# A graph network on one core: the column table and the attention weights of the attention loops stand in PSUM

## The chip, the cores and the metric

The kernel runs on one core of a Trainium2 chip. A core has a matrix engine (TensorE, PE in the profile), a vector engine (VectorE, DVE), a scalar engine (ScalarE, ACT), a general engine (GpSimd, POOL) and a queue engine (SyncE, SP). Each works off its own instructions in order and waits on semaphores for the others. SBUF is the working memory; PSUM is the small memory that TensorE writes its products into, in eight banks of 512 float32 values for each of 128 partitions. The metric is the device time of one execution in microseconds, and the figure compared is the median over runs.

## The reference

Four layers work on a graph of 3125 nodes with 256 features. Each layer adds a graph part, a mixing part (linear attention over all nodes) and a feed-forward part to the node features. The graph parts of layers 0 and 2 are graph attention over 50,000 edges sorted by destination, with 4 and 8 heads. Cut to what matters:

```
def _L2_gnn_ref(x, edge_index, W, att_src, att_dst, ...):
    xl = (x @ W).reshape(n, H, C)
    a_src = jnp.einsum('nhc,hc->nh', xl, att_src)
    a_dst = jnp.einsum('nhc,hc->nh', xl, att_dst)
    ...                                   # every node is an edge to itself too
    logits = jax.nn.leaky_relu(a_src[src] + a_dst[dst], 0.2)
    seg_max = jax.ops.segment_max(logits, dst, num_segments=n)
    ex = jnp.exp(logits - seg_max[dst])
    denom = jax.ops.segment_sum(ex, dst, num_segments=n)
    alpha = ex / denom[dst]
    msgs = xl[src] * alpha[:, :, None]
    out = jax.ops.segment_sum(msgs, dst, num_segments=n).reshape(n, H * C) + bias
    ...                                   # layer norm over the features
```

The other layers' graph parts are a weighted sum over the edges (layer 1, twice) and three rounds of sums (layer 3).

## The kernel before

Nodes stand in 25 blocks of 128 rows. Edges stand in 416 tiles of 128, each tile within one block of destinations; `self.blk` holds the block of each tile and `self.dl` the place of each edge's destination in its block. Four tiles make a group (`G = 4`), two groups a pair (`Z = 2`), so an attention loop runs over 104 groups, or 52 pairs.

The method `gat` (line 746) does one attention layer. Per group `g` its loop runs these steps; `k` is the number of the pair.

- `fetch(g)` (line 849) issues four gathers on GpSimd (line 533), which bring 128 rows of the table `htab` each from memory into a buffer `msg` of SBUF. There are five such buffers.
- `terms(k)` (line 817) loads a row of destinations, builds a transposed one-hot matrix `ohT` on VectorE (line 823) and copies eight rows of destination terms to `stage` on ScalarE (line 828), each from an offset read from `blk`.
- `look(k, i)` (line 830) multiplies the two on TensorE, four small matmuls per call (line 834), into the PSUM tile `pds[k % 2]`, one bank for even pairs and one for odd ones.
- `weights(k)` (line 837) sums the three bfloat16 parts on VectorE (line 841), forms the logits `z` there (lines 843 to 845) and takes the exponential on ScalarE (line 847) into `alpha`, a tile of SBUF.
- `scale(g)` (line 856) multiplies the gathered messages by `alpha` in place (line 860), copies `alpha` beside them (line 861), and builds the one-hot matrix `oh` of the destinations (`one_hot`, line 537, its instruction on line 540), which compares `dl` with a table of the column numbers 0 to 127, `self.cols`. All three are VectorE's and all operands are in SBUF.
- `sums(g)` (line 865) multiplies `oh` by the messages on TensorE, four matmuls (line 871) into two PSUM buffers named `g`; `add_to` (line 546) adds each product to the block's row of `agg` on VectorE, one group later.

In a turn with an even `g` the pair's steps stand in front of the group's: `weights(k + 1)`, then `terms(k + 2)`; each turn then issues `look(k + 2, g % 2)`, `scale(g)`, `sums(g)` and the additions of the group before. Between turns a generator `steps` issues parts of the mixing computation (matmuls of lines 467, 465 and 504 with their ScalarE and VectorE work), which fill TensorE beside the loop.

The order of the instructions on each engine is not that of the text: a scheduler orders them when the kernel is built, by its own costs, and sets the semaphores. It tracks dependences inside a PSUM tile by bank. Two instructions of different engines that touch one bank of one tile, in which at least one of them writes, are put in order and wait for each other, though they touch different columns.

Layer 1 has a loop of the same make, `gather_sum` (line 552). It runs twice, over the table `c_tab`. In its second run the comparison takes the column table from a PSUM tile named `acc`, and its other long VectorE instructions have an operand in PSUM as well.

Of the kernel before, what the change touches and what calls it, by code (L numbers as in the profile page):

```python
# [9 lines left out]
F32 = mybir.dt.float32  # L10
# [9 lines left out]
P = 128  # L20
# [10 lines left out]
G = 4  # L31
# [20 lines left out]
def bc(ap, shape):  # L52

    idx, full = [], []
    own = list(ap.shape)
    for n in shape:
        if n is None:
            idx.append(slice(None))
            full.append(own.pop(0))
        else:  # L60
            idx.append(None)
            full.append(n)
    assert not own
    return ap[tuple(idx)].to_broadcast(full)


class Net:
# [678 lines left out]
    def gat(self, pool, pre, H, tiny, side, deg=None, after=None, during=None):  # L746

        nc, tc = self.nc, self.tc
# [56 lines left out]
        Z = 2  # L805
        ng = NS // G
        state = {}
        heads = agg[:, :, :D].rearrange("p t (h c) -> p t h c", h=H)
        with ExitStack() as own:
            steps = side(own)  # L810
            msgs = own.enter_context(self.pool("msgs", 5))
            ps = own.enter_context(self.pool("gat_ps", 1, PSUM))

            pds = [ps.tile([P, Z * G, 2, H, 3], F32, name=f"pd{i}") for i in range(2)]

            def terms(k):

                t0, n = k * Z * G, Z * G
                dr = pool.tile([P, n, P], BF16, name="dr")
                rows = self.dl_rows[t0:t0 + n]  # L820
                nc.sync.dma_start(dr, bass.AP(tensor=rows.tensor, offset=rows.offset, ap=[[0, P], [P, n], [1, P]]))
                ohT = pool.tile([P, n, P], BF16, name="ohT")
                nc.vector.tensor_scalar(ohT, dr, self.row, None, op0=ALU.is_equal)
                pd = pds[k % 2]
                rows = pool.tile([P, n, 6 * H], BF16, name="stage")
                for j in range(n):
                    at = self.block_of(t0 + j, ET.Activation) * (6 * H)
                    nc.scalar.copy(rows[:, j, :], dmf[:, bass.ds(at, 6 * H)])  # L828
                state["pd", k] = pd, ohT, rows

            def look(k, i):
                pd, ohT, rows = state["pd", k]
                for j in range(i * G, (i + 1) * G):
                    nc.tensor.matmul(pd[:, j].rearrange("p s h k -> p (s h k)"), ohT[:, j, :], rows[:, j, :],  # L834
                                     start=True, stop=True)

            def weights(k):
                t0, n = k * Z * G, Z * G
                pd4 = state.pop(("pd", k))[0]
                pd = pool.tile([P, n, 2, H], F32, name="pds")  # L840
                nc.vector.tensor_reduce(pd, pd4, axis=AX.X, op=ALU.add)
                z = pool.tile([P, n, H], F32, name="z")
                nc.vector.tensor_tensor(z, ase[:, t0:t0 + n, :], pd[:, :, 0, :], ALU.add)
                nc.vector.scalar_tensor_tensor(z, z, 0.2, z, op0=ALU.mult, op1=ALU.max)
                nc.vector.tensor_tensor(z, z, pd[:, :, 1, :], ALU.subtract)
                al_ = pool.tile([P, n, H], F32, name="alpha")
                nc.scalar.activation(al_, z, AF.Exp)
                state["w", k] = al_

            def fetch(g):  # L850
                msg = msgs.tile([P, G, W], F32, name="msg")
                for j in range(G):
                    self.gather(msg[:, j, :D], htab, g * G + j)
                state["msg", g] = msg

            def scale(g):
                msg = state["msg", g]
                al_ = state["w", g // Z][:, (g % Z) * G:(g % Z + 1) * G, :]
                mh = msg[:, :, :D].rearrange("p j (h c) -> p j h c", h=H)
                nc.vector.tensor_tensor(mh, mh, bc(al_, [None, None, None, C]), ALU.mult)  # L860
                nc.vector.tensor_copy(msg[:, :, D:D + H], al_)
                if deg is not None:
                    nc.vector.memset(msg[:, :, D + H:], 1.0)
                state["oh", g] = self.one_hot(pool, g)

            def sums(g):
                oh, msg = state.pop(("oh", g)), state.pop(("msg", g))
                out = []
                for j in range(G):
                    q = ps.tile([P, 512], F32, name="g", bufs=2)[:, :W]  # L870
                    nc.tensor.matmul(q, oh[:, j, :], msg[:, j, :], start=True, stop=True)  # L871
                    out.append(q)
                state["q", g] = out

            terms(0)
            look(0, 0)
            look(0, 1)
            weights(0)
            terms(1)
            look(1, 0)  # L880
            look(1, 1)
            nc.scalar.activation(ws, ws, AF.Exp)
            nc.vector.tensor_tensor(heads, heads, bc(ws, [None, None, None, C]), ALU.mult)
            nc.vector.tensor_copy(agg[:, :, D:D + H], ws)
            if deg is not None:
                nc.vector.memset(agg[:, :, D + H:], 0.0)
            for g in range(ng + 1):
                if g < ng:
                    fetch(g)
                    k = g // Z  # L890
                    if g % Z == 0:
                        if k + 1 < ng // Z:
                            weights(k + 1)
                        if k + 2 < ng // Z:
                            terms(k + 2)
                    if k + 2 < ng // Z:
                        look(k + 2, g % Z)
                    scale(g)
                    sums(g)
                if g:  # L900
                    self.add_group(agg, g - 1, state.pop(("q", g - 1)))
                if g % 6:
                    next(steps, None)
                if g < ng and during is not None:
                    during(g)
            for _ in steps:
                pass
# [10 lines left out]
        for b in range(0, NB, BB):  # L918
            s = slice(b, b + BB)
# [1583 lines left out]
```

## Time and profile before

| what | value |
|---|---|
| median of 6 runs | 6624.34 us (6580.49 to 6642.68) |
| the profiled execution, its own time | 6648.39 us |
| its span on the core | 6646.6 us |
| mean granted clock of TensorE | 0.849 |
| attention loop of layer 0 | about 572 to 1180 us of the span |
| attention loop of layer 2 | about 4055 to 4710 us of the span |
| second loop of layer 1, column table in PSUM | about 2380 to 3190 us |

The page has a busy time for each engine, a strip of 40 slices, the chain of work that ended last, and groups of instructions with their mean time and what ended the idle time before them. In a group's row, `msg<-msg,alpha` is output and inputs by the program's names; the figure behind the bar is the busy time in microseconds, then the mean of one instruction in nanoseconds, then the idle time before them and its releasers. `issue` is idle time for which no releaser is seen, and `remote` a releaser that the profile does not name.

### The profile page before, as it was taken

How to read it: one execution, taken by the hardware profiler on the slowest of the kernel's cores; microseconds unless marked ns; L12 is line 12 of the kernel's file. 1: busy time of each engine (PE TensorE's matmuls, PEld its weight loads, DVE VectorE, ACT ScalarE, POOL GpSimd, SP SyncE). 2: the span in 40 equal slices, each digit the busy share in tenths (PEclk: the TensorE clock that was granted, in tenths of full speed). 3: DMA queues.
4: the chain of work that ended last, by engine and by line, in shares of the span. 5: the costliest groups of instructions: out<-in, count | busy, mean ns of one | idle time of the engine just before them, and what ended most of it. 6: DMA issues, size and time to landing. Idle time of an engine off the chain costs nothing.

```text
span 6646.6 us, 82827 instructions
## 1 busy us (share of the span) xinstructions
PE 4809.2 (72%) x25818; PEld 3420.4 (51%) x25818; DVE 3259.6 (49%) x8397; ACT 1691.2 (25%) x4750; POOL 2334.4 (35%) x2289
## 2 busy tenths in 40 slices
PE   2364766397576565665577765777799999998897
PEld 1112334375355433444366322444576788787796
DVE  6146766725477646777634445666853200124222
ACT  1012213322100034554322212231444310111232
POOL 1605776421556625555131525666100000002111
PEclk9687888598778777777688887888899999999898
DMA  3362333254222313333145322333111232122644
GB/s 98 101 186 65 110 107 101 81 189 135 88 67 77 90 50 119 130 129 123 61 159 189 89 83 66 105 103 101 38 45 61 74 139 85 64 75 90 223 172 161
DMA packets 380559, 702.63 MB, mean 106 GB/s; under 512 B 100052, under 2 KB 220062, under 8 KB 380114
## 3 DMA queue, kind: packets, MB, share of 16 engines
q1 hardware_dynamic: 264293, 424.36, 19.4%
q0 software_dynamic: 105664, 263.07, 13.3%
q10 hardware_dynamic: 10157, 9.80, 0.4%
q8 instruction: 214, 3.51, 0.2%
q14 instruction: 231, 1.89, 0.1%
HBM read 568.63 MB, written 128.36 MB: 105 GB/s over the span
## 4 chain that ended last, share of the span: by engine, by line
PE 32%; issue 8%; DVE 4%; POOL 3%; another core or an unknown queue 2%; DMA 2%; ACT 1%; SPq 0%; DVEq 0%; ACTq 0%; POOLq 0%
PE dn L2209 12%; PE mm L467 4%; PE g L871 2%; PE h L1521 2%; PE mm L504 2%; PE y L1534 2%; PE q L666 1%; PE mm L1808 1%; POOL msg L533 1%; PE mm L2267 1%; PE q L675 1%; POOL back L1538 1%; PE mm L458 1%; DVE agg L546 0%
## 5 line engine op out<-in xcount | busy, mean ns | idle before, releaser
L533 POOL DMA_INDIRECT msg<-L_gnn_htab,src x832 | 899.1, 1081 | 596.1 <-issue 224.4
L533 POOL DMA_INDIRECT msg<-L_gnn_c_tab,src x832 | 820.0, 986 | 772.3 <-issue 452.5
L546 DVE TENSOR_TENSOR agg<-agg,g 128x256 f32 (+2 forms) x1664 | 700.2, 421 | 578.8 <-remote 229.0
L594 PE MATMUL g<-msg,oh 128*128 128x256 f32 x1664 | 579.1, 493 | 319.1 <-DVE agg L546 126.5
L2209 PEld LDWEIGHTS <-a 128*128 128x128 bf16 x7500 | 734.6, 98 | 126.2 <-issue 39.1
L871 PE MATMUL g<-msg,oh 128*128 128x261 f32 (+1 forms) x1664 | 589.2, 462 | 239.5 <-DVE agg L546 142.1
L1416 POOL DMA_INDIRECT sent<-xs,ids x150 | 152.9, 1019 | 1548.8 <-DVE pos L1409 1396.0
L594 PEld LDWEIGHTS g<-msg,oh 128*128 128x128 f32 x1664 | 374.7, 244 | 480.6 <-DVE agg L546 163.7
L871 PEld LDWEIGHTS g<-msg,oh 128*128 128x128 f32 x1664 | 323.9, 218 | 501.3 <-DVE agg L546 244.2
L1521 PE MATMUL h<-xe,w 128*128 128x128 f32 x3584 | 435.5, 277 | 5.3 <-DMA w<-in_L_ffn_W 5.0
L1538 POOL DMA_INDIRECT back<-y,toi x168 | 163.2, 971 | 782.4 <-DVE y L1537 515.9
L2209 PE MATMUL dn<-hb,a 128*128 128x256 bf16 x3750 | 424.8, 274 | 9.9 <-issue 9.5
L1534 PE MATMUL y<-w,hT 128*128 x1792 | 431.2, 388 | 0.0
L2209 PE MATMUL dn<-ha,a 128*128 128x256 bf16 x3750 | 423.3, 273 | 5.3 <-ACT ha L2178 5.1
L1521 PEld LDWEIGHTS h<-xe,w 128*128 128x128 f32 x3584 | 420.6, 194 | 7.0 <-DVE toi L1510 3.7
L1525 ACT ACTIVATE hT<-h,br 128x128 f32<-128x128 f32 x896 | 255.6, 368 | 660.4 <-issue 570.6
L1534 PEld LDWEIGHTS y<-w,hT 128*128 128x128 f32 x1792 | 326.6, 190 | 57.0
L828 ACT COPY stage<-dm 128x24 bf16 (+1 forms) x832 | 182.9, 221 | 579.0 <-PE pd L834 172.0
L1537 DVE COPY y<-y 128x256 f32<-128x256 f32 x168 | 71.2, 424 | 525.3 <-PE y L1534 525.1
L666 PE MATMUL q<-ohl,t 128*104 128x512 bf16 (+1 forms) x702 | 196.5, 409 | 120.1 <-DVE pr L672 65.3
L533 POOL DMA_INDIRECT ase<-tab,src x208 | 213.7, 1028 | 150.8 <-PE q L666 85.9
L567 ACT ACTIVATE msg<-msg,ew 128x256 f32<-128x256 f32 x416 | 199.0, 506 | 265.8 <-DMA msg<-L_gnn_c_tab,src 238.9
(705 smaller groups left out, 7644.8 us busy)
## 6 DMA issues: line engine op xcount, KB each, us to landing
a<-counted SPq DMA_DIRECT2D x100, 800.0 KB
w<-in_L_ffn_W SPq DMA_DIRECT2D x128, 512.0 KB
w<-in_L_ffn_W SPq DMA_DIRECT2D x64, 1024.0 KB
counted<-T SPq DMA_DIRECT2D x40, 800.0 KB
dr<-dl_rows SPq DMA_DIRECT2D x104, 256.0 KB
sent<-zeros SPq DMA_DIRECT2D x25, 1040.0 KB
xr<-sent SPq DMA_DIRECT2D x168, 130.0 KB
lw<-lo_rows SPq DMA_DIRECT2D x78, 256.0 KB
```

The lines of the kernel that those rows point to most:

```text
L467: nc.tensor.matmul(q, xT[:, k, t * P:(t + 1) * P], w[:, k, cols], start=(k == 0 and bias is None), stop=(k == nk - 1))
L533: self.nc.gpsimd.indirect_dma_start(out=out, out_offset=None, in_=table, in_offset=bass.IndirectOffsetOnAxis(ap=self.src[:, t:t + 1], axis=0))
L546: self.nc.vector.tensor_tensor(at, at, q, ALU.add)
L567: nc.scalar.mul(msg[j], msg[j], self.ew[:, g * G + j:g * G + j + 1])
L594: self.summed = self.nc.tensor.matmul(r, oh[:, j, :], msg[j], start=True, stop=True)
L666: nc.tensor.matmul(q[:M], t3[:, k, i, :], oh[:, k, :], start=((k, i) == mm[0]), stop=((k, i) == mm[-1]))
L871: nc.tensor.matmul(q, oh[:, j, :], msg[:, j, :], start=True, stop=True)
L1521: nc.tensor.matmul(q[:, i, :], d["w1"][:, k, c * P:(c + 1) * P], d["xe"][:, k, :], start=(k == 0), stop=(k == 1))
L1525: nc.scalar.activation(hT[:, c, :], q[:, i, :], act, bias=d["br"][:, c:c + 1])
L1534: nc.tensor.matmul(q, d["hT"][:, c, :], w2f[:, bass.ds(e * (nh * D) + c * D, D)], start=False, stop=(c == nh - 1))
L1538: s = nc.gpsimd.indirect_dma_start(out=self.back, out_offset=bass.IndirectOffsetOnAxis(ap=d["to"][:, 0:1], axis=0), in_=y, in_offset=None)
L2209: nc.tensor.matmul(q, a[:, k, :], h[:, k, i, :], start=(k == 0 and i == 0), stop=(k == NB - 1 and i == 2))
```

## The change

The two tiles `pd0` and `pd1` become whole banks of 512 columns. The products of `look` keep the first `8 * 6 * H` columns (192 with 4 heads, 384 with 8). The last 128 columns of the first bank take a copy of the column table, made once before the loop on ScalarE; `one_hot` compares with it. The last 128 columns of the second bank take `alpha`, 64 columns for even and 64 for odd pairs, where it was a new SBUF tile for each pair.

```
-            pds = [ps.tile([P, Z * G, 2, H, 3], F32, name=f"pd{i}") for i in range(2)]
+            banks = [ps.tile([P, 512], F32, name=f"pd{i}") for i in range(2)]
+            nw = Z * G * 6 * H
+            pds = [b[:, :nw].rearrange("p (j s h k) -> p j s h k", j=Z * G, s=2, h=H) for b in banks]
+            table = banks[0][:, 384:]
+            nc.scalar.copy(table, self.cols)
+            alphas = [banks[1][:, 384 + i * 64:384 + i * 64 + Z * G * H].rearrange("p (j h) -> p j h", h=H)
+                      for i in range(2)]
...
-                al_ = pool.tile([P, n, H], F32, name="alpha")
+                al_ = alphas[k % 2]
                 nc.scalar.activation(al_, z, AF.Exp)
...
-                state["oh", g] = self.one_hot(pool, g)
+                state["oh", g] = self.one_hot(pool, g, table)
```

## The prediction

> **What bounds the kernel now.** I read the page first, then the busy times of three stretches, then the waits of VectorE and of GpSimd in the two attention loops, then the groups of GpSimd in the loop of layer 1 that already has its table in PSUM. The change touches nothing outside the attention loops, 608 + 655 = 1263 us of 6646.6.
>
> ```profile
> span 6646.6 us, 82827 instructions
> L533 POOL DMA_INDIRECT msg<-L_gnn_htab,src x832 | 899.1, 1081 | 596.1 <-issue 224.4
> L871 PE MATMUL g<-msg,oh 128*128 128x261 f32 (+1 forms) x1664 | 589.2, 462 | 239.5 <-DVE agg L546 142.1
> ```
>
> The busy times of the two attention loops and of that other loop (length, PE, weight loads, DVE, ACT, POOL, clock, DMA share, GB/s):
>
> ```profile
> 572.00:1180.00 608.00, 440.20 (x1628) 243.28 (x1629) 425.93 (x1127) 168.64 (x538) 429.62 (x390) 0.84 0.35 105
> 4055.00:4710.00 655.00, 501.10 (x1934) 305.62 (x1935) 442.15 (x1123) 170.74 (x672) 425.54 (x398) 0.88 0.35 102
> 2380.00:3190.00 810.00, 495.59 (x2304) 327.81 (x2303) 528.09 (x753) 402.38 (x1102) 393.31 (x416) 0.76 0.34 112
> ```
>
> Three engines are about 70% busy and none is full: TensorE 72 and 77%, VectorE 70 and 68%, GpSimd 71 and 65%. GpSimd's gathers, by loop (layer 0, layer 2, second loop of layer 1):
>
> ```profile
> L533 POOL DMA_INDIRECT msg<-L_gnn_htab,src x390 | 429.6, 1102 | 197.9 <-issue 104.7 <-PE g L871 71.3 <-remote 10.8
> L533 POOL DMA_INDIRECT msg<-L_gnn_htab,src x396 | 425.3, 1074 | 233.3 <-PE g L871 113.0 <-issue 107.2 <-remote 8.4
> L533 POOL DMA_INDIRECT msg<-L_gnn_c_tab,src x416 | 393.3, 945 | 419.8 <-issue 239.9 <-DMA L_gnn_c_tab<-hb 116.0 <-ACT msg L567 33.8
> ```
>
> One gather takes 945 ns where every long VectorE instruction has a PSUM operand, and 1102 and 1074 ns in the attention loops, where the scaling (1.22 us) and the comparison (0.68 us) have two SBUF inputs. In the timeline a gather that meets a scaling is the long one: 1.96 us at 712.43, beside a scaling from 712.35. So the change does reach something. But who waits for gathers? VectorE in layer 0, then in layer 2:
>
> ```profile
> DVE agg L546 <- remote: 63.2, 21, 5.9
> DVE agg L546 <- PE g L871: 51.2, 64, 6.4
> DVE agg L546 <- PE mm L467: 16.4, 10, 5.5
> DVE agg L546 <- PE pd L834: 11.6, 6, 3.7
> DVE msg L860 <- DMA msg<-L_gnn_htab,src: 6.9, 4, 2.8
> ...
> DVE agg L546 <- PE g L871: 99.1, 88, 5.2
> DVE agg L546 <- remote: 66.5, 21, 7.5
> DVE agg L546 <- PE mm L467: 20.7, 16, 2.6
> ```
>
> The scaling, the first reader of the messages, waits for a gather for 6.9 us in layer 0; in layer 2 no such line appears. The other way round GpSimd waits 71.3 and 113.0 us for TensorE to free a buffer. TensorE and VectorE are the loop's limit: a product waits for an addition (60.7 and 77.8 us of TensorE's waits), an addition for a product, with two buffers between them. "Remote" at the additions is most likely TensorE too, some of whose records are missing; I count it as such.
>
> **The change, part by part.**
>
> *Gathers.* (1102 - 945) x 390 = 61 us and (1074 - 945) x 396 = 51 us of GpSimd's time may go, 112 in all, or less, as the bfloat16 comparison of line 823 and the small ones of lines 843 to 845 keep their SBUF operands. GpSimd is not what the loop waits for, so the freed time becomes longer waits for a buffer. On the path I take what VectorE waited for messages: -7 us. Bounds: 0 and -112.
>
> *VectorE's own durations.* The comparison with the table in PSUM is a row of this trace: 681 ns against 684, over 208 of them -0.6 us. A copy of 16 values from PSUM (line 772) takes 175 ns and the copy of `alpha` from SBUF 175: nothing. The scaling with one PSUM operand has no row; by the comparison's pair of rows I take no difference. One ScalarE copy of 128 columns for each loop is 0.27 us (the row of `acc<-cols`). Sum -0.1 us; I take 0, by bounds of -3 and +17 ns (one step up in the row of 8 and 16 values is 8 ns) over 624 instructions: -2 to +11 us, partly in idle time.
>
> [...]
>
> *New waits.* The two banks now hold what VectorE reads as well as what TensorE writes, and the order of the changed kernel shows what that costs. The eight matmuls of `look`, which stood in one run, are split four and four with waits between. In each loop 48 scalings wait for a set of these matmuls, 18 and 13 comparisons do; 29 and 36 sets wait for a comparison, 24 and 17 for the copy of `alpha`, 26 for the exponential. And nearly every pair (51 of 52) has a scaling behind the exponential that was just issued, as both use the second bank; before, that exponential was needed a pair (11.7 us) later. What stands behind each: behind a set on TensorE, products and mixing matmuls; behind a scaling on VectorE, the additions that TensorE's next products wait for.
>
> Exponential: in layer 2's timeline it starts a median 0.11 us behind its `z` and takes 0.25, so with the way back 0.11 + 0.25 + 0.11 = 0.47 us. In the new order VectorE has a median of 1.10 us (layer 0) and 0.83 us (layer 2) of other work between `z` and the scaling, by the instructions that stand between and their rows. That hides it, except where ScalarE reloads its function table (1283 ns in the page's rows; 15 + 2 pairs by the new order): 1.28 + 0.47 - 1.10 = 0.65 us, 17 times, +11 us. If the cover went it would be 0.47 x 104 = 49 us.
>
> Odd pairs: the set stands between exponential and scaling, four matmuls of 0.25 us by the run of eight (0.47 us), so 0.47 + 0.25 + 0.11 = 0.83 us. In 55 of 102 pairs the cover is under 1.0 us, mostly 0.42 or 0.69; half are odd: 27 x 0.25 = +7 us.
>
> Run-ahead: while TensorE was late, VectorE could do the next scaling, copy and comparison (1.22 + 0.17 + 0.68 us). Now a scaling stands behind TensorE. VectorE's waits for TensorE above are 143 us in 101 waits (24% of the loop) and 186 us in 125 (28%), 1.4 us each. A quarter of 48 scalings, 12 per loop, fall into one and lose half of it: 12 x 0.7 x 2 loops = +17 us. Bounds: 0, and 48 x 1.4 x 2 = +134 us.
>
> TensorE: 79 waits per loop for VectorE or ScalarE ahead of a set, at least a hop of 0.11 us: 79 x 2 x 0.11 = 17 us, half of it in waits that were there: +8 us. Bounds 0 and 79 x 2 x 0.5 = 79.
>
> **Sum**: -7 + 0 + 11 + 7 + 17 + 8 = +36 us, 2.9% of the two loops. From the profiled execution, 6648.4 us, that is 6684; it ran 24 us above the median of the runs, so against the median 6624 + 36 = 6660 us, +0.5%.
>
> **The rivals.**
>
> *Gathers decide (faster).* Place: GpSimd's queue in both loops. A gather and the 0.30 us behind it take 390 x 1.40 = 546 of 608 us and 396 x 1.37 = 544 of 655: 90 and 83% full, near enough to a limit to starve the scaling in bursts that the wait list books elsewhere. If half of the 112 us comes to the path: 6624 - 56 = 6568. It decides if more than 43 us (36 + 7) of the loops' time hangs on messages. For it: 90%. Against: 6.9 us of waits, and buffers that are full for 71 and 113 us.
>
> *The waits all fall into idle time, and the gain too.* VectorE and TensorE idle by 28% already, and the scheduler placed the new waits behind other work: 6624. For it: the median covers above. Against: the sets behind the second bank, with 0.42 us.
>
> *Exponentials come late (much slower).* In layer 0's timeline an exponential starts 3.79 us (mean) behind its `z`, in layer 2 0.96, as ScalarE first does the copies to `stage` in front. If that stayed, each pair would lose 3.79 + 0.25 + 0.11 - 1.10 = 3.05 us in layer 0 and 0.96 + 0.25 + 0.11 - 0.83 = 0.49 in layer 2: 52 x 3.54 = +184, 6808. Half of it: 6716. Against: in the new order no `stage` copy stands between the sum of the parts and the exponential in 43 of 52 pairs of layer 0, where eight stood in 28 of 52 before.
>
> **How the numbers follow.** About 0.5% (33 us) is what a measurement can tell from no change. My forecast 0.42 (6630 to 6700; 0.30 of it slower by over 0.5%, 0.12 within); waits and gain both hidden 0.20 (within); gathers decide 0.22 (0.19 faster, 0.03 within); late exponentials 0.16 (slower). So faster 0.19, within 0.35, slower 0.46. The range 6580 to 6740 leaves out half of the gathers' case and about a third of the last, 0.16. The forecast alone: 6630 to 6700.
>
> **What would show it.** Gathers at 945 to 980 ns in both loops; GpSimd's waits for TensorE's product up by 50 us or so per loop; comparison 681 ns, scaling about 1.22 us. New lines: scaling waits for the exponential and for `pd`, TensorE's `pd` for VectorE. The loops 610 to 640 and 660 to 690 us long. I am wrong if the loops are shorter than before, if gathers stay over 1050 ns, or if the scaling's wait for the exponential exceeds 50 us.

## The result, and the profile after

The changed kernel takes 6657.81 us (median of 37 runs, 6597.11 to 6694.41), the kernel before, run beside it, 6619.59 us (79 runs). The ratio is 1.0054, 95% interval 1.0037 to 1.0070: slower by 0.5%, some 36 us. The profiled execution of the changed kernel took 6657.46 us. It is only 9 us longer than that of before, which lay 29 us above the median of its runs, so the two profiles must be compared stage by stage.

The runs fell into two kinds of session, "long" ones, in which the kernel before takes 6620 to 6644 us, and "short" ones, in which it takes 6118 to 6127 us, and one and the same chip showed both. The result above and the profile that the prediction was made from are of long sessions. Every ratio below is against the kernel before in the same session.

Lines of the changed kernel's page (a group's row: busy us, mean ns of one, idle us before, and its releaser):

```profile
span 6655.7 us, 82804 instructions
L533 POOL DMA_INDIRECT msg<-L_gnn_htab,src x832 | 792.9, 953 | 723.9 <-PE g L879 251.1
L879 PE MATMUL g<-msg,oh 128*128 128x261 f32 (+1 forms) x1664 | 599.3, 469 | 225.3 <-DVE agg L546 117.1
L868 DVE TENSOR_TENSOR msg<-msg,pd 128x1024 f32<-128x1024 f32 x208 | 253.1, 1217 | 102.2 <-issue 28.0
```

Gathers fell from 1081 to 953 ns. The scaling, now line 868, lasts 1217 ns, no longer than with SBUF operands (1219), but 102 us of idle time stand in front of it. A matmul instruction of a product (each product has two) takes 469 ns on average where it took 462.

The two attention loops of the changed kernel, from the first scaling to the last addition (length, then busy time of PE, weight loads, DVE, ACT, POOL; clock, DMA share, GB/s):

```profile
583.70:1220.30 636.60, 471.03 (x1685) 255.93 (x1685) 444.67 (x1171) 166.21 (x531) 379.13 (x397) 0.85 0.34 101
4053.90:4719.40 665.50, 514.82 (x1937) 306.65 (x1937) 444.65 (x1121) 167.33 (x657) 375.77 (x398) 0.87 0.34 101
```

Cut in the same way, the loops of before are 571.30 to 1203.10 and 4057.00 to 4711.70, that is 631.8 and 654.7 us, with TensorE busy for 457.98 and 502.33, VectorE for 444.99 and 443.40 and GpSimd for 435.66 and 425.54 us. So GpSimd lost 106 us of work, and the loops became 4.8 and 10.8 us longer. VectorE's idle time grew by 15 us (398 to 413). TensorE's fell by 10 us (326 to 316), while its busy time, for the same instructions, grew by 26 (960 to 986), as more of it was spent at half clock (348 us of both loops before, 374 after).

VectorE's waits in the loop of layer 0 and in that of layer 2 of the changed kernel (us, times, longest):

```profile
DVE agg L546 <- PE g L879: 62.6, 72, 4.9
DVE agg L546 <- remote: 43.8, 21, 4.2
DVE msg L868 <- remote: 13.2, 4, 3.8
DVE msg L868 <- PE g L879: 11.9, 6, 2.8
DVE msg L868 <- ACT pd L855: 8.1, 5, 4.3
...
DVE msg L868 <- DMA msg<-L_gnn_htab,src: 4.5, 2, 3.8
DVE msg L868 <- PE pd L842: 3.8, 6, 1.9
```

```profile
DVE agg L546 <- PE g L879: 74.0, 77, 4.0
DVE agg L546 <- remote: 29.8, 13, 4.4
DVE msg L868 <- issue: 24.6, 17, 3.8
...
DVE msg L868 <- remote: 13.3, 3, 7.3
```

In the prediction's lists of before, nearly all of VectorE's waiting stood at `agg`, the addition. Part of it has moved to `msg`, the scaling: idle time in front of the scalings is 102 us in both loops together (16 before), while that in front of the additions fell from 362 to 282 us.

The profiles also show a difference ahead of the loops, and it comes out the same in every profile of the two kernels. From the addition of `none` to `mx` (line 781) to the first scaling, before takes 17.3 us in layer 0 and 18.4 in layer 2, the changed kernel 21.2 and 22.8. The weights of pair 0 and of pair 1 stand in one bank, and the exponential of pair 1 is issued ahead of the first scaling, which waits until it is over. In the timeline of layer 0 (the exponentials are line 855):

```profile
575.77 0.19 ACT L855 ACTIVATE pd<-z 128x32 f32<-128x32 f32 x1
...
583.47 0.19 ACT L855 ACTIVATE pd<-z 128x32 f32<-128x32 f32 x1
583.70 1.22 DVE L868 TENSOR_TENSOR msg<-msg,pd 128x1024 f32<-128x1024 f32 x1 [4.25 <-ACT pd L855]
```

The second exponential ends at 583.66 us, the scaling starts at 583.70, 7.7 us after the end of the exponential that it needs. The preparation is thus 3.9 and 4.4 us longer, which the prediction did not have.

### The profile page after: what moved, and what is told of

Same layout as the page of the kernel before. It is cut to its first block, busy times and chain, and to the rows that moved or that the text cites. A ratio compares the mean times of both kernels' runs of the same rounds, so it can differ in the third digit from the quotient of the medians.

```text
span 6655.7 us, 82804 instructions
## 1 busy us (share of the span) xinstructions
PE 4826.5 (73%) x25818; PEld 3414.5 (51%) x25818; DVE 3266.8 (49%) x8397; ACT 1685.5 (25%) x4748; POOL 2225.3 (33%) x2289
## 4 chain that ended last, share of the span: by engine, by line
PE 31%; issue 9%; DVE 4%; POOL 3%; another core or an unknown queue 2%; DMA 2%; ACT 1%; SPq 0%; DVEq 0%; ACTq 0%; POOLq 0%
PE dn L2217 12%; PE mm L467 4%; PE g L879 2%; PE h L1529 2%; PE mm L504 2%; PE y L1542 2%; PE q L666 1%; PE mm L1816 1%; PE mm L2275 1%; POOL msg L533 1%; PE q L675 1%; POOL back L1546 1%; PE mm L458 1%; DVE agg L546 1%
## 5 line engine op out<-in xcount | busy, mean ns | idle before, releaser
L533 POOL DMA_INDIRECT msg<-L_gnn_htab,src x832 | 792.9, 953 | 723.9 <-PE g L879 251.1
L868 DVE TENSOR_TENSOR msg<-msg,pd 128x1024 f32<-128x1024 f32 x208 | 253.1, 1217 | 102.2 <-issue 28.0
```

Of the source, the lines that this page charges most:

```text
L533: self.nc.gpsimd.indirect_dma_start(out=out, out_offset=None, in_=table, in_offset=bass.IndirectOffsetOnAxis(ap=self.src[:, t:t + 1], axis=0))
```

## The experiments

### One part of the change at a time (a long session, before 6644.26 us)

Theory: the loss is what the shared banks cost; the shorter gathers are worth nothing, as the loop does not wait for messages. Rivals: the gathers are worth something and the waits eat it; reading PSUM is itself dear.

Only the table in PSUM:

```
-            alphas = [banks[1][:, 384 + i * 64:384 + i * 64 + Z * G * H].rearrange("p (j h) -> p j h", h=H)
-                      for i in range(2)]
...
-                al_ = alphas[k % 2]
+                al_ = pool.tile([P, n, H], F32, name="alpha")
```

> Only the column table moves to PSUM (first bank); the attention weights stay in SBUF. Sharing theory (what cost the 36 us is that VectorE's operands stand in banks that TensorE writes): the comparison is one of the two operands, and only 18 and 13 comparisons waited for a set of matmuls, so a small part of the loss, +5 to +15 us against before; gathers somewhat shorter, 1040 to 1080 ns, as only the comparison (0.68 us per group) leaves SBUF. Relief theory (gathers are worth something and the waits on the attention weights eat it): -10 to -30 us. Operand theory (PSUM reads themselves are dear): the comparison over 700 ns and the time over +15 us.

Measured: 6621.93 us, ratio 0.9983 (0.9952 to 1.0015), no difference that can be told from none. The interval, -32 to +10 us, holds parts of both theories' ranges and decides between neither. Gathers 1072 and 1065 ns in the two loops.

Only the weights in PSUM:

```
-            table = banks[0][:, 384:]
-            nc.scalar.copy(table, self.cols)
...
-                state["oh", g] = self.one_hot(pool, g, table)
+                state["oh", g] = self.one_hot(pool, g)
```

> Only the attention weights move to PSUM (second bank); the column table stays in SBUF. Sharing theory: nearly the whole loss, +20 to +40 us against before, with the scaling's new waits for the exponential, for the small matmuls and for remote of about 20 us per loop each or less; gathers 980 to 1010 ns. Relief theory: gathers near 990 ns bring something back, -10 to +10 us. Operand theory: the scaling over 1230 ns.

Measured: 6725.35 us, ratio 1.0115 (1.0070 to 1.0160), twice the loss of the whole change, and more than the 20 to 40 us expected. Gathers 976 and 969 ns, the scaling 1216 ns (1219 before). So the instruction is not slower for its operand, and the gathers' relief is nearly all there.

The weights crossed over the banks, so that no scaling stands behind the exponential of its own turn:

```
-            alphas = [banks[1][:, 384 + i * 64:384 + i * 64 + Z * G * H].rearrange("p (j h) -> p j h", h=H)
-                      for i in range(2)]
+            alphas = [banks[1 - i][:, 384:384 + Z * G * H].rearrange("p (j h) -> p j h", h=H) for i in range(2)]
```

> Only the attention weights move to PSUM, but those of an even pair stand in the second bank and those of an odd pair in the first, so that a scaling does not share its bank with the exponential issued in its own pair's turn. Sharing theory: the scaling's wait for the exponential goes, the waits of the small matmuls stay in part: +5 to +25 us against before, less than with the weights all in the second bank. Relief theory: -10 to -30 us. Rival (which bank it is does not matter, the loss is in having PSUM operands or in another order of the instructions): the same time as with the weights all in the second bank, within 8 us.

Measured: 6672.25 us, ratio 1.0052 (1.0023 to 1.0082). The idle time in front of the scalings is gone, and the preparation is 3.1 and 2.1 us shorter than before. About half of the loss of the weights went, but half stayed, although no scaling waits any more. (The table is in SBUF here too.)

The weights in PSUM, but read there only by the small copy; the scaling takes the copy from SBUF (the table is in SBUF here too):

```
-                nc.vector.tensor_tensor(mh, mh, bc(al_, [None, None, None, C]), ALU.mult)
                 nc.vector.tensor_copy(msg[:, :, D:D + H], al_)
+                nc.vector.tensor_tensor(mh, mh, bc(msg[:, :, D:D + H], [None, None, None, C]), ALU.mult)
```

> The weights stand in PSUM as in the changed kernel, but only the small copy beside the messages reads them there; it is made before the scaling, which then reads that copy in SBUF. All waits between the banks' users remain, the relief of the gathers is gone (two SBUF inputs again: 1080 to 1110 ns). Sharing theory with a relief that is worth nothing: the same time as with the weights in PSUM and read there, within 8 us, +20 to +40 us against before. If the relief of the gathers brings time that the waits hide: slower than that by 10 us or more.

Measured: 6645.34 us, ratio 1.0015 (0.9988 to 1.0043). This misses the theory, by which it should have cost as much as the weights read in place. The same instructions share the bank in it, and the gathers are long again (1058 and 1084 ns), yet the time is that of before within the interval. One thing that differs is how long the bank is held: 0.17 us by the copy instead of 1.22 + 0.17 us by scaling and copy. TensorE's waits in the two kernels, first the weights read in place (layer 0, layer 2), then read by the copy (layer 0; in layer 2 such waits come to 0.2 us):

```profile
PE pd L840 <- DVE msg L867: 23.2, 8, 7.0
...
PE pd L840 <- DVE msg L867: 28.6, 11, 7.3
```

```profile
PE pd L840 <- DVE msg L869: 10.2, 1, 10.2
PE pd L840 <- DVE msg L866: 8.5, 4, 4.8
```

The small matmuls wait 52 us for VectorE to leave the bank in the one and 19 us in the other, and VectorE idles 169 us in front of the scalings in the one, 105 in front of copies and scalings in the other. This points to a long VectorE instruction that holds a bank which TensorE has to write next as what cost time in a long session. It is not shown alone: the two kernels also differ in where the scaling reads the weights and in how long the gathers are, and the crossed kernel, with hardly any of these waits, still has half of the loss.

### A second profile of each, the supply, and the clock (a short session, before 6120.91 us)

The first two are the two kernels unchanged. They were meant to test a clock theory: that the changed waits crowd TensorE's idle time so that its clock drops.

> The kernel before, profiled a second time, to see how far a loop's length and TensorE's granted clock vary from one execution to the next. In the four variants so far and in both profiles at hand the two loops together differ by TensorE's busy time more than by its idle time: before 1286.5 us long with TensorE busy 960.3 and idle 326.2, changed 1302.1 with 985.9 and 316.2. Clock theory (the changed waits crowd TensorE's idle time into stretches that drop its clock to half): this profile repeats 1280 to 1293 us and 953 to 968 us busy, a time at half clock of 335 to 365 us in both loops. Chance theory (the difference is the scatter of executions): 1295 us or more, or 980 us busy or more.

> The changed kernel, profiled a second time. Clock theory: the two loops together 1295 to 1315 us, TensorE busy 978 to 992 us, idle 308 to 325 us, 360 to 395 us at half clock; from the start of the loop's preparation to the first scaling 3.9 and 4.4 us longer than before, as in the first profile. Chance theory: below 1290 us, or busy below 970 us.

Measured: 6122.08 us for the kernel before and 6036.49 us for the changed one, one execution each: here the change is faster. The two loops together take 1134 and 1050 us, far outside what the clock theory expected, and neither theory had a reason for that. The changed kernel was timed beside before once more, in another short session. (The expectation speaks of chips; that one chip gives both kinds of session was seen afterwards.)

> The changed kernel against the kernel before, both on one chip. Late-product theory (on the chips of 6620 us TensorE's products come late in some 37 spells per loop and are the loop's limit; on the chip of 6121 us none comes late and the messages are the limit): if the kernel before takes about 6120 us here, the changed one is 70 to 100 us faster, its scalings' waits for messages down from 59 and 63 us per loop to 30 us or less, no product over 1 us late; if the kernel before takes about 6620 us, the changed one is 25 to 50 us slower, with 25 or more products over 1 us late in each loop. Rival (the one execution of 6036 us was an accident, the change costs half a per cent everywhere): slower on a chip of 6120 us too.

Measured: 6045.40 us (4 runs) against 6126.57 (7 runs), ratio 0.9869 (0.9852 to 0.9885): 81 us faster. The change has the opposite sign in the two kinds of session, with the same gathers (957 ns) and the same instructions.

The kernel before in the short session: two rows of its page, and VectorE's waits in the loop of layer 0 and of layer 2:

```profile
L533 POOL DMA_INDIRECT msg<-L_gnn_htab,src x832 | 893.7, 1074 | 384.1 <-issue 217.9
...
L860 DVE TENSOR_TENSOR msg<-msg,alpha 128x1024 f32<-128x1024 f32 x208 | 254.3, 1222 | 136.6 <-DMA msg<-L_gnn_htab,src 122.3
```

```profile
DVE msg L860 <- DMA msg<-L_gnn_htab,src: 59.4, 33, 3.4
DVE agg L546 <- PE g L871: 48.2, 86, 5.6
...
DVE msg L860 <- DMA msg<-L_gnn_htab,src: 63.0, 37, 3.8
DVE agg L546 <- PE g L871: 50.3, 81, 2.3
```

Against the lists of the long session two things are reversed. The releaser `remote`, 63.2 and 66.5 us there, does not occur in front of VectorE's instructions in these loops. And the scaling waits 59 and 63 us for messages, where it waited 6.9 us and not at all. The loops are 568.6 and 565.8 us long instead of 631.8 and 654.7.

What the `remote` waits are can be seen in the timeline of before in the long session, around 657 us (start, duration, engine, line, instruction, idle time before it):

```profile
657.00 0.60 PE L871 MATMUL g<-msg,oh 128*128 128x261 f32 x2
657.91 0.95 POOL L533 DMA_INDIRECT msg<-L_gnn_htab,src  x1 [0.30 <-issue]
...
661.47 0.43 DVE L546 TENSOR_TENSOR agg<-agg,g 128x261 f32 x1 [4.22 <-remote]
...
661.82 1.22 DVE L860 TENSOR_TENSOR msg<-msg,alpha 128x1024 f32<-128x1024 f32 x1
661.96 1.14 PE L871 MATMUL g<-msg,oh 128*128 128x261 f32 x2 [4.35 <-issue]
```

The product's matmuls end at 657.6 by the record, whose ends are modelled, but the addition that needs them starts 3.9 us later. In the trace, TensorE's semaphore steps at 658.57, 660.01 and 661.45, and the addition starts at 661.47: the product really came late. Meanwhile GpSimd goes on gathering at its usual pace, 0.95 us a gather and 0.30 us between two. Over both loops 64 additions start over 1 us behind the modelled end of their product after VectorE has idled for over 1 us, in the long session (56 in the changed kernel there); in the short session none does, in either kernel. So in a long session TensorE is the limit of the loop and messages lie ready; in a short one TensorE keeps up and messages are the limit.

Why products come late in some sessions stays open, but the traces tell two things more. The three steps above lie 1.44 us apart. In both loops of the long session 77 recorded steps of TensorE's semaphore follow the one before by 1.39 to 1.48 us, against 15 in the short session, and 166 by 0.41 to 0.48 us, against 453; the clock record has full clock (1.0) from 621.1 to 662.1 us. So TensorE delivers more slowly in these spells than its clock record explains. And the profiles of the six long sessions' runs hold 42,900 to 44,300 steps of semaphores, those of the eight short ones 72,300 to 75,900. Part of the record is missing in the long ones; whether the recording itself has a part in the lateness no run here tests. The lateness is not confined to these loops: the stage between 180 and 375 us of the long session, with matmuls of line 666 and 675, takes 195 us, and the same stage 78 us in the short one.

VectorE's waits in the changed kernel, in the short session beside which it took 0.9869, layer 0:

```profile
DVE agg L546 <- PE g L879: 38.2, 71, 2.9
DVE msg L868 <- DMA msg<-L_gnn_htab,src: 16.3, 13, 2.2
DVE msg L868 <- ACT pd L855: 9.1, 9, 4.3
DVE msg L868 <- PE pd L842: 3.8, 9, 1.1
```

The wait for messages fell from 59.4 to 16.3 us (63.0 to 6.5 in layer 2), and the new waits cost less than that. The loops are 518.0 and 526.0 us long.

To see what the supply alone is worth, one gather in four was left out of the kernel before (`bufs` are five fixed tiles, zeroed once before the loop):

```
-                msg = msgs.tile([P, G, W], F32, name="msg")
-                for j in range(G):
+                msg = bufs[g % 5]
+                for j in range(G - 1):
                     self.gather(msg[:, j, :D], htab, g * G + j)
```

> The kernel before with five fixed message buffers, of whose four rows of tiles only three are gathered; the fourth keeps what stood in it, so the gathers' work, 430 us of GpSimd per loop, falls by a quarter, as much as the changed kernel took off it (56 and 50 us) twice over, and no bank is shared. If GpSimd does not limit the loop: within 15 us of before, GpSimd's waits for TensorE's product up by 80 us or more per loop. If it does (the rival of the prediction in which gathers decide): 40 us or more faster.

Measured: 5984.38 us, ratio 0.9779 (0.9766 to 0.9793): 137 us faster, by the rival's expectation. Its page:

```profile
L533 POOL DMA_INDIRECT msg<-L_gnn_htab,src x624 | 699.2, 1121 | 398.1 <-PE g L874 218.5
...
L863 DVE TENSOR_TENSOR msg<-msg,alpha 128x1024 f32<-128x1024 f32 x208 | 253.4, 1218 | 8.1 <-ACT alpha L850 8.1
```

No scaling waits for a message any more, and GpSimd waits for TensorE instead. So by this run about 140 us can be had in a short session by relief of the gathers, and the change gets 81.

One more small matmul behind each product, to keep TensorE busy (`banks` as in the change, here with their last columns free):

```
...
                     nc.tensor.matmul(q, oh[:, j, :], msg[:, j, :], start=True, stop=True)
+                    nc.tensor.matmul(banks[(g // Z) % 2][:, 384:], dmf[:, :P], dmf[:, :P], start=True, stop=True)
```

> The kernel before with one more small matmul behind each product of the loop, 128 columns of bfloat16 into a free part of the pd banks that nobody reads: 416 per loop, about 0.06 to 0.11 us each, 25 to 45 us of TensorE per loop, part of it in idle time. Clock theory: TensorE is busier in each stretch of 3.4 us, the time at half clock falls below the 197 and 152 us of before by 40 us or more in all, and the g products' mean of 462 ns falls below 450; the time within 20 us of before, or faster. If the clock has no part in the loops' length: the clock as before and 30 to 80 us slower.

Measured: 6133.02 us, ratio 1.0023 (1.0012 to 1.0033). The time at half clock fell by 39 us (235 to 196 in both loops), a matmul instruction of a product from 453 to 446 ns, TensorE was busy for 29 us more, and the kernel is 12 us slower. So the clock rose as the clock theory expected, and the time did not fall with it: in a short session, a higher clock bought with more work brought nothing. The clock theory for the long session was not tested by this.

### Parts again, in short sessions

> The changed kernel with the weights of even pairs in the second bank and of odd pairs in the first in both loops; the table stays in PSUM in layer 0 only, since in layer 2 the first bank has no room for both. Late-product theory: no scaling waits behind the exponential of its own turn, so the preparation before the first scaling is 3 us shorter than before instead of 4 longer; on a chip of 6120 us 70 to 110 us faster than before and within 25 us of the changed kernel; on a chip of 6620 us 0 to 40 us slower than before. Rival (the sharing of a bank is what costs, wherever the products stand): faster than the changed kernel by 20 us or more on either chip.

```
-            table = banks[0][:, 384:]
-            nc.scalar.copy(table, self.cols)
-            alphas = [banks[1][:, 384 + i * 64:384 + i * 64 + Z * G * H].rearrange("p (j h) -> p j h", h=H)
-                      for i in range(2)]
+            alphas = [banks[1 - i][:, 384:384 + Z * G * H].rearrange("p (j h) -> p j h", h=H) for i in range(2)]
+            if H == 4:
+                table = banks[0][:, 256:384]
+                nc.scalar.copy(table, self.cols)
+            else:
+                table = self.cols
```

Measured, in the same session as the repeated changed kernel: 6048.05 us, ratio 0.9866 (0.9850 to 0.9883), the same as the changed kernel (0.9869). The preparation is 7 us shorter per loop (14.2 and 16.3 us), the loop of layer 2 lost some gather relief (980 ns instead of 954), and its 533.7 us are 7.7 us longer than the changed kernel's. Crossing the banks brings nothing in all.

The weights read by the copy, the edit as above:

> The weights in PSUM, read there only by the small copy, the scaling from the copy in SBUF: all waits of the shared bank, no relief of the gathers. Late-product theory: on a chip of 6120 us the relief was the whole gain, so this one is not faster than before, 0 to 30 us slower, gathers 1060 to 1090 ns and the scalings' waits for messages 40 us or more per loop; on a chip of 6620 us within 20 us of before, as in its first run. Rival (the gain on the chip of 6120 us came from another order of the instructions, not from the gathers): 40 us or more faster than before on a chip of 6120 us.

Measured: 6136.69 us against 6118.24, ratio 1.0032 (1.0021 to 1.0043). Its scalings wait 35 and 45 us for messages, with gathers of 1087 ns. So the waits of the shared bank cost 18 us without the relief (some 8 of them are the longer preparation, which this kernel has too), and the gain of the change doesn't come from another order of the instructions.

The weights read in place, the edit as above:

> The weights in PSUM and the column table in SBUF. Late-product theory: on a chip of 6120 us the gathers, at 970 to 980 ns, keep about nine tenths of the relief and the time is 50 to 85 us shorter than before; on a chip of 6620 us it is 40 to 90 us longer again, the longest of all variants, since its scalings hold the second bank and stand behind TensorE. Rival (the shared second bank costs the same 70 us on every chip): within 20 us of before on a chip of 6120 us.

Measured: 6078.04 us, same session, ratio 0.9936 (0.9921 to 0.9951): 40 us faster than before, somewhat less than expected. Its waits, layer 0:

```profile
DVE msg L866 <- ACT pd L853: 16.2, 10, 3.6
DVE msg L866 <- DMA msg<-L_gnn_htab,src: 12.6, 10, 2.9
```

The ratios side by side:

| kernel | long session | short session |
|---|---|---|
| the change | 1.0054 (1.0037 to 1.0070) | 0.9869 (0.9852 to 0.9885) |
| weights only | 1.0115 (1.0070 to 1.0160) | 0.9936 (0.9921 to 0.9951) |
| weights only, read by the copy | 1.0015 (0.9988 to 1.0043) | 1.0032 (1.0021 to 1.0043) |
| weights only, crossed | 1.0052 (1.0023 to 1.0082) | not run |
| table only | 0.9983 (0.9952 to 1.0015) | not run |
| table and weights, crossed | not run | 0.9866 (0.9850 to 0.9883) |

The third row shares the bank and has no relief: +10 us, not to be told from 0, and +18 us. From it to the second, the scaling reads the weights in the bank, which takes 0.1 us off each gather: it is worth 59 us in a short session (6136.69 to 6078.04) and costs 80 by the medians in a long one (6645.34 to 6725.35). With the table added, the change does better than the weights alone in both kinds of session, though the table alone brings nothing that can be told from none in a long one; no run explains that. No variant was faster than before in a long session by more than its interval; the changed kernel and the crossed one share the best time in a short one.

## Why the prediction was right or wrong

The time, 6657.8 against 6660 us, is right for the kind of session that the profile at hand was taken in. Its steps hold in part, and that the sum is within 2 us is luck: the two loops grew by 15.6 us where the sum has 36, and the rest of the difference is a term that it lacks and 14 us that could not be placed. In a short session the loops are shorter than before, which the prediction named as a sign of being wrong, and there it is.

*What bounds the loop.* TensorE and VectorE, not GpSimd: right in the long session, where the scalings' waits for messages stayed at 7 to 8 us although the gathers got 0.1 us shorter. The `remote` waits were TensorE, as the prediction took them, but not for want of matmul records: all 832 of each loop are there, and the products came late. (The 143 us of waits that the prediction counts in layer 0 add up to 142.4, which changes nothing.)

*Gathers, -7 us.* They became as short as predicted (957 and 949 ns for 945), GpSimd lost 106 us of work (112). On the path it was 0 in the long session, 6.9 us of waits becoming 8.2. In the short session, where the kernel became 81 us faster in spite of what the shared banks cost, the term is some -81 us or more, nearer to the step's other bound of -112.

*VectorE's durations, 0.* Right: scaling 1217 ns (mean of 208, before 1219), comparison 680 ns where it was 684.

*Table reloads, +11 us.* The scalings' wait for the exponential came to 12.7 us; 8.3 of it stand in front of the two first scalings, so it is 4.4 us within the loops. The exponential starts 0.86 and 0.35 us behind its `z` (means; 3.79 and 0.96 before). The order hid it as argued, and the rival of late exponentials fell.

*Odd pairs, +7, and run-ahead, +17 us.* The mechanism is there: the scalings stand behind TensorE's matmuls, with 86 us more of idle time in front of them in both loops (of the 102 us, 23 end with a matmul by name, 26 are `remote`, and for 28 no releaser is seen). The term was mis-sized, since it counted the waits as added and they mostly moved: a late product that used to hold up an addition now holds up the scaling ahead of it, and idle time in front of the additions fell by 80 us (362 to 282). With the reloads these three terms make 35 us; VectorE's idle time grew by 15.

*TensorE's hops, +8 us.* The small matmuls wait 45 us where they waited 1.2, but TensorE's idle time as a whole fell by 10; the longer loops show as 26 us more busy time at a lower clock. The term can't be seen by itself.

*What was missing.* The preparation, +8.3 us. Loops and preparation make +24 us between the two profiles; the medians differ by 38. The remaining 14 us could not be placed: the stretch from the end of the first loop to the start of the second, which the change touches in the preparation alone, is 20 us shorter in the changed kernel's execution.

*What stays open.* In long sessions the three kernels whose scaling reads PSUM are slower, even the crossed one with no wait in front of its scalings, and the two whose scaling reads SBUF are not, as far as can be told. For the one with its bank in the way (weights only) TensorE's 52 us of waits are probably part of it. In the crossed one TensorE's new waits for a bank come to some 4 us in layer 0, three exponentials wait 17.5 us for a scaling, and the clock is lower (399 us at half clock in both loops, 348 before). Whether there the scaling's reads of PSUM or the shorter gathers make TensorE slower was not told apart.

*The rival "gathers decide"* had the right place and price (90% full, waits in front of the scaling, half of 112 us or more) and was rejected by one row, 6.9 us of waits for messages. That row is right, but belongs to one kind of session; in the other it reads 122 us, above the 43 us from which this rival was to decide, and the change gains 81 us. So the step that does not carry over is "GpSimd is not what the loop waits for".

## What to carry to other kernels

Relief for an engine is worth what the loop waits for that engine's product, and this wait can be 7 us in one session and 122 in another of the same kernel: the loops of this kernel, with three engines at about 70%, had TensorE for a limit in one and the messages in the other, so a second profile, from another session, is worth more there than a finer sum over one wait. Before an operand is moved into a bank that TensorE writes, ask how long its reader will hold the bank: held for 0.17 us it cost nothing that could be measured in a long session, held for 1.4 us it went with a loss of 1%, part of which has another cause. In this kernel `remote` in front of the additions was TensorE being late, and its absence in the second profile told which limit held.

## What the runs showed of the hardware

- A gather takes 1081 ns (mean) beside scalings of 128x1024 and comparisons of 128x512 with two SBUF inputs, and 953 ns where both have one input in PSUM. The table in PSUM alone brings 1068 ns, the weights alone 973.
- In a long session VectorE idled up to 7.5 us behind the modelled end of a product that it needed, in spells; in the short ones never by more than 1 us. One chip showed both kinds of session (before 6644.26 and 6126.57 us).
- The clock record of these profiles has full clock (1.0) and half clock (0.5), and changes in steps of 3.41 us. In both loops of the long session's two profiles, before and changed, a stretch of 3.41 us at full clock in which matmuls fill less than 40%, by their modelled ends, is followed by half clock in 67 of 67 cases, one filled to 60% or more in 4 of 391. Back from half clock the bar is higher: below 80% filled, 72 of 73 stretches are followed by half clock again, from 90% on 8 of 116. An estimate from these counts puts the two bars near 50% on the way down and 85% on the way up. A matmul instruction of a product lasts 386 ns (median, modelled end) when it starts at the one clock and 644 (before) or 647 ns (changed) at the other.
